# The first feed-forward product of eight layers, computed by seven products of quarters per pair of chunks

## The chip, the core and the metric

The kernel runs on one core of a Trainium2 chip. The core has a matrix engine (TensorE, in the profile PE, with its weight loads as PEld), a vector engine (VectorE, DVE), an engine for activation functions (ScalarE, ACT), a general one (GpSimd, POOL) and one that issues transfers (SyncE, SP). Each engine works through its own queue in order, and they wait for one another by semaphores. Operands lie in SBUF, products in PSUM, which has eight banks; a bank holds 512 float32 values in each of 128 partitions. The metric is the device time of one execution, in microseconds (us). Everything is float32.

## What is computed

The program is a perceiver block over 512 latent rows of 512 features: attention to 8192 context rows, eight transformer layers with an attention that is linear in length, and a feed-forward part with selected experts. The change touches the eight layers. One of them is, in the reference:

```python
def _block(x, p):
    residual = x
    q = jnp.einsum('nld,da->nla', x, Wq) + bq
    k = jnp.einsum('nld,da->nla', x, Wk) + bk
    v = jnp.einsum('nld,da->nla', x, Wv) + bv
    Q = jax.nn.elu(q) + 1.0
    K = jax.nn.elu(k) + 1.0
    KV = jnp.einsum('nsh,nsh->nh', K, v)
    Ksum = jnp.sum(K, axis=1)
    Z = 1.0 / (Q * Ksum[:, None, :] + EPS_Z)
    V = Q * KV[:, None, :] * Z
    attn = jax.nn.gelu(jnp.einsum('nla,ad->nld', V, Wo) + bo)
    x = _layernorm(attn + residual, ln1_s, ln1_b)
    residual = x
    h = jax.nn.gelu(jnp.einsum('nld,df->nlf', x, Wf1) + bf1)
    ff = jax.nn.gelu(jnp.einsum('nlf,fd->nld', h, Wf2) + bf2)
    x = _layernorm(ff + residual, ln2_s, ln2_b)
    return (x, None)
```

The line that changes is `h`: 512 tokens with 512 features each, times `Wf1` with 512 rows and 2048 columns.

## The kernel before

After the attention to the context (lines 135 to 565) the layers run one after the other (loop at line 724). Each layer has three stages on the matrix engine: the products for k, q and v with the output projection (lines 765 to 781), the first feed-forward product (line 795), and the second one (lines 805 to 811). The order of the matrix engine's instructions is that in which the code issues them; the other engines' orders are made by a scheduler that follows the data.

**The first product.** Its result is held by features: `hT[fc]`, for 16 chunks `fc`, has 128 features in the partitions and 512 tokens in the columns. The input `midT` holds the tokens' features in four slices `dc` of 128 partitions. `feature` (line 624) computes one chunk, or some columns of it: for each of the four slices a matmul with a 128x128 piece of `w_1` as weights and the tokens as moving operand, summed in PSUM. One such float32 matmul shows in the trace as two records of the matrix engine and two weight loads. `hidden` (line 786) then has ACT apply gelu from PSUM into `hT`.

**Its order.** `midT` comes into being while the product runs. The rows that the output projection leaves are normalized (`finish`, line 668), transposed by the matrix engine and copied into `midT` by ACT (`turn`, line 693), one block of 128 tokens at a time, by four calls for blocks 0 to 3. So `features` (line 631) starts with five chunks held in PSUM: of these it computes 128 tokens, or 256, as the blocks arrive, with the three remaining transposes put in between, and the other eleven chunks follow with 512 columns at a time.

**Around it.** `affine` (line 689) computes the normalized rows themselves, `mid`, on DVE: two instructions per block of tokens, right after the last `finish`. They are read by the `finish` of the second product (line 807). The second product, `returned` (line 704), takes for each block of tokens all 16 chunks of `hT` in order.

**Buffers.** PSUM is shared out as five banks for products (`mm`) and three for sums and transposes (`acc`), lines 595 and 596. The residual rows `cur` and their transposed form `curT` have two buffers each, which `mid` and `midT` take in turn; `cur` is read last by the `finish` of the output projection, `curT` by the product for v. The weights of the following stages are loaded by SP as the buffers of earlier ones come free (`layer_weights`, line 569), the rows of biases and scales by ACT's queue (line 729).

Of the kernel before, what the change touches and what calls it, by code (L numbers as in the profile page):

```python
# [8 lines left out]
F32 = mybir.dt.float32  # L9
I32 = mybir.dt.int32  # L10
AF = mybir.ActivationFunctionType
ALU = mybir.AluOpType
# [4 lines left out]
P = 128  # L17
# [3 lines left out]
TT = T // P  # L21
# [10 lines left out]
NF = DFF // P  # L32
# [8 lines left out]
C_BF1 = 112  # L41
# [4 lines left out]
R_BO, R_S1, R_B1, R_BF2, R_S2, R_B2 = range(6)  # L46
# [8 lines left out]
def perceiver_kernel(  # L55
# [3 lines left out]
    nc = tc.nc  # L59
# [17 lines left out]
    col = cpool.tile([P, NCOL], F32, name="col")  # L77
# [76 lines left out]
    def bank(name, shape=None):  # L154
        return ps_s.tile(shape or [P, BLK], F32, tag="s", name=name)
# [56 lines left out]
    k_sb, v_sb, xT, part, rows_of, trigs = {}, {}, {}, {}, {}, {}  # L212
# [118 lines left out]
    while min(met) < NCHUNK:  # L331
        p = k % NPAIR
# [261 lines left out]
    with ExitStack() as s_:  # L594
# [36 lines left out]
        def features(chunks, xT, turns, done):  # L631


            held = [(mm.tile([P, T], F32, tag="mm", name="ps"), *c) for c in chunks[:EARLY]]

            def tile_of(t, chunks_):
                for i in chunks_:
                    ps, w, c0 = held[i]
                    feature(ps, w, c0, xT, t * P, P)
                    if t % 2:  # L640
                        done(i, ps, (t - 1) * P, H)

            def half(t0, chunks_):
                for i in chunks_:
                    ps, w, c0 = held[i]
                    feature(ps, w, c0, xT, t0, H)
                    done(i, ps, t0, H)

            if 1 in turns:
                tile_of(0, (0, 1))  # L650
                turns[1]()
                tile_of(0, (2,))
                tile_of(1, (0, 1, 2))
            else:
                half(0, (0, 1, 2))
            half(0, (3,))
            turns[2]()
            half(0, (4,))
            turns[3]()
            tile_of(2, (0, 1))  # L660
            tile_of(3, (0, 1))
            half(H, (2, 3, 4))
            for i, (w, c0) in enumerate(chunks[EARLY:], EARLY):
                ps = mm.tile([P, T], F32, tag="mm", name="ps")
                feature(ps, w, c0, xT)
                done(i, ps, 0, T)

        def finish(ps, old, bias, t, eng):

            g = gpool.tile([P, D], F32, tag="g", name="g")  # L670
            nc.vector.tensor_tensor(g, ps, bias, ALU.add)  # L671
            nc.scalar.activation(g, g, AF.Gelu_apprx_tanh)  # L672
            nc.vector.tensor_tensor(g, g, old[:, t, :], ALU.add)
            mv = small.tile([P, 1, 2], F32, tag="mv1", name="mv")
            st = small.tile([P, 6], F32, tag="st", name="st")
            nc.vector.bn_stats(st, g)
            nc.vector.bn_aggr(mv[:, 0, :], st)
            r = rsqrt_of(mv[:, :, 1], 1, 1e-6)
            if eng is None:
                return g, mv[:, 0, 0:1], r  # L680
            if eng is nc.vector:
                last = nc.vector.tensor_scalar(g, g, mv[:, 0, 0:1], r, ALU.subtract, ALU.mult)
            else:
                n = small.tile([P, 1], F32, tag="nmr1", name="nmr")
                last = nc.vector.scalar_tensor_tensor(n, mv[:, 0, 0:1], -1.0, r, ALU.mult, ALU.mult)
                nc.scalar.activation(g, g, AF.Identity, bias=n, scale=r)
            return g, last

        def affine(dst, g, scale, shift):
            nc.vector.tensor_tensor(dst, g, scale, ALU.mult)  # L690
            nc.vector.tensor_tensor(dst, dst, shift, ALU.add)
# [32 lines left out]
        for l in range(NL):  # L724
            w_k, w_q, w_v, w_o, w_1, w_2 = layer_weights(l) if l else first
            row = []
            for i in range(6):
                rt = rpool.tile([P, D], F32, tag="row", name=f"row{l}_{i}", bufs=9)
                nc.scalar.dma_start(out=rt, in_=rows[l, i].partition_broadcast(P))
                row.append(rt)  # L730


            kf, ksum, qf, y, vt = {}, {}, {}, {}, {}

            def taken(i, ps, t0, n):
                ac = i % DC
                ts = slice(t0, t0 + n)
                ps = ps[:, ts]
                if i < DC:
                    if t0 == 0:  # L740
                        kf[ac] = fea.tile([P, T], F32, tag="k", name="kf")
                        ksum[ac] = small.tile([P, 3], F32, tag="ksum", name="ksum", bufs=6)
                    k = ksum[ac]
                    elu1(ps, C_BK + l * DC + ac, kf[ac][:, ts], k[:, t0 // H : t0 // H + 1])
                    if t0:
                        nc.vector.tensor_tensor(k[:, 2:3], k[:, 0:1], k[:, 1:2], ALU.add)
                elif i < 2 * DC:
                    if t0 == 0:
                        qf[ac] = fea.tile([P, T], F32, tag="q", name="qf", bufs=2)
                    elu1(ps, C_BQ + l * DC + ac, qf[ac][:, ts])  # L750
                    if t0 + n == T:
                        y[ac] = fea.tile([P, T], F32, tag="y", name="y")
                        nc.vector.tensor_scalar(y[ac], qf[ac], ksum[ac][:, 2:3], 1e-6, ALU.mult, ALU.add)
                        nc.vector.reciprocal(y[ac], y[ac])  # L754
                        nc.gpsimd.tensor_tensor(y[ac], qf[ac], y[ac], ALU.mult)  # L755
                else:
                    c = C_BV + l * DC + ac
                    kvs = small.tile([P, 1], F32, tag="kvs", name="kvs")
                    nc.vector.scalar_tensor_tensor(
                        kf[ac], ps, col[:, c : c + 1], kf[ac], ALU.add, ALU.mult, accum_out=kvs  # L760
                    )
                    nc.vector.tensor_scalar(y[ac], y[ac], kvs, None, ALU.mult)
                    vt[ac] = y[ac]

            chunks = [(w, ac * P) for w in (w_k, w_q, w_v) for ac in range(DC)]
            features(chunks, curT, turns, taken)


            mid = cpl.tile([P, TT, D], F32, tag="cur", name="mid")
            midT = cpl.tile([P, DC, T], F32, tag="curT", name="midT")  # L770
            c1, c2 = (C_S1 + l * DC, C_B1 + l * DC), (C_S2 + l * DC, C_B2 + l * DC)
            gs = {}
            for t in range(TT):
                po = acc.tile([P, D], F32, tag="acc", name=f"po_{l}_{t}")
                for ac in range(DC):
                    if t == TT - 1 and ac == 2:
                        turn(midT, gs[0], 0, *c1)
                    nc.tensor.matmul(  # L778
                        po, vt[ac][:, t * P : (t + 1) * P], w_o[:, ac, :], start=(ac == 0), stop=(ac == DC - 1)
                    )  # L780
                gs[t], last = finish(po, cur, row[R_BO], t, nc.scalar)
            turns = {t: lambda dst=midT, g=gs[t], t=t, c=c1: turn(dst, g, t, *c) for t in (1, 2, 3)}

            hT = {}

            def hidden(fc, ps, t0, n):
                if t0 == 0:
                    hT[fc] = hpool.tile([P, T], F32, tag="h", name="h")
                ts = slice(t0, t0 + n)
                c = C_BF1 + l * NF + fc  # L790
                nc.scalar.activation(  # L791
                    hT[fc][:, ts], ps[:, ts], AF.Gelu_apprx_tanh, bias=col[:, c : c + 1]
                )

            features([(w_1[fc // 4], (fc % 4) * P) for fc in range(NF)], midT, turns, hidden)

            with tc.issue_after(last.ins):
                for t in range(TT):
                    affine(mid[:, t, :], gs[t], row[R_S1], row[R_B1])

            cur = cpl.tile([P, TT, D], F32, tag="cur", name="cur")
            if l + 1 == NL:
                break
            curT = cpl.tile([P, DC, T], F32, tag="curT", name="curT")
            for t in range(TT):
                pf = returned(t, range(NF))
                gs[t], last = finish(pf, mid, row[R_BF2], t, nc.vector)
                affine(cur[:, t, :], gs[t], row[R_S2], row[R_B2])
                if t and t < 3:
                    turn(curT, gs[t - 1], t - 1, *c2)  # L810
            turns = {t: lambda dst=curT, g=gs[t], t=t, c=c2: turn(dst, g, t, *c) for t in (2, 3)}
# [265 lines left out]
```

## Time and profile before

| | us |
|---|---|
| median of 3 runs (lowest, highest) | 2690.72 (2688.86, 2693.32) |
| the profiled execution, its own time | 2689.87 |
| its span in the profile | 2688.0 |
| PE busy | 2621.7 (98% of the span) |
| DVE busy | 1482.6 (55%) |
| ACT busy | 1127.0 (42%) |
| POOL busy | 778.5 (29%) |
| first product, first layer (1298.58 to 1355.70) | 57.12 |
| second product, first layer (1355.70 to 1410.70) | 55.00 |
| next layer's k, q, v and output projection (1410.70 to 1471.40) | 60.70 |

The lower three rows are stretches of the matrix engine's work, cut at the first record of each stage. An engine's busy time is the union of its instructions; matmuls are pipelined, so the mean duration of one is longer than the distance from one to the next. "Released by" names the instruction whose semaphore ended an idle time. Over the whole program POOL works mainly in the attention to the context; in the layers it has one kind of instruction, four times a layer (line 755).

### The profile page before, as it was taken

How to read it: one execution, taken by the hardware profiler on the slowest of the kernel's cores; microseconds unless marked ns; L12 is line 12 of the kernel's file. 1: busy time of each engine (PE TensorE's matmuls, PEld its weight loads, DVE VectorE, ACT ScalarE, POOL GpSimd, SP SyncE). 2: the span in 40 equal slices, each digit the busy share in tenths (PEclk: the TensorE clock that was granted, in tenths of full speed). 3: DMA queues.
4: the chain of work that ended last, by engine and by line, in shares of the span. 5: the costliest groups of instructions: out<-in, count | busy, mean ns of one | idle time of the engine just before them, and what ended most of it. 6: DMA issues, size and time to landing. Idle time of an engine off the chain costs nothing.

```text
span 2688.0 us, 27832 instructions
## 1 busy us (share of the span) xinstructions
PE 2621.7 (98%) x9704; PEld 1264.3 (47%) x9704; DVE 1482.6 (55%) x2892; ACT 1127.0 (42%) x2125; POOL 778.5 (29%) x642
## 2 busy tenths in 40 slices
PE   8999999999999999979999999999999999999998
PEld 4433333433343333335546555455554555645544
DVE  4467677776767776876428055271461623706344
ACT  2466566565666666652314233133231331413303
POOL 0356666666765666760000000000000000100002
PEclk9999999999999999989999999999999999999999
DMA  3111111110111111105213222032221322212225
GB/s 132 48 44 40 39 37 30 53 37 27 45 42 38 34 40 40 40 7 178 76 68 103 71 90 90 31 121 90 74 90 47 115 81 86 79 63 94 68 91 202
DMA packets 98347, 187.10 MB, mean 70 GB/s; under 512 B 10336, under 2 KB 10464, under 8 KB 98208
## 3 DMA queue, kind: packets, MB, share of 16 engines
q1 hardware_dynamic: 88496, 167.29, 19.4%
q10 hardware_dynamic: 8688, 15.94, 1.8%
q0 software_dynamic: 1024, 2.10, 0.2%
q8 instruction: 77, 1.26, 0.2%
q14 instruction: 62, 0.51, 0.1%
HBM read 162.22 MB, written 1.05 MB: 61 GB/s over the span
## 4 chain that ended last, share of the span: by engine, by line
PE 71%; DVE 17%; ACT 5%; issue 4%; POOL 2%; DMA 0%; SPq 0%; DVEq 0%; POOLq 0%; ACTq 0%
PE ps L626 20%; PE pf L708 16%; PE pv L259 7%; PE pk L230 6%; PE po L455 6%; PE pc L374 6%; DVE y L754 4%; DVE sc L434 3%; PE po L778 3%; ACT sc L377 2%; ACT sc L435 1%; POOL es L445 1%; DVE qf L620 1%; PE pt L218 1%; DVE mx L383 1%
## 5 line engine op out<-in xcount | busy, mean ns | idle before, releaser
L445 POOL TENSOR_TENSOR es<-es,sc 128x1024 f32<-128x1024 f32 x222 | 524.9, 2365 | 114.7 <-ACT sc L435 103.7
L626 PE MATMUL ps<-midT,w 128*128 128x512 f32 (+2 forms) x1664 | 451.7, 431 | 0.0
L708 PE MATMUL pf<-w,h 128*128 128x512 f32 x1024 | 444.5, 593 | 0.0
L755 POOL TENSOR_TENSOR y<-qf,y 128x512 f32<-128x512 f32 x32 | 47.0, 1468 | 1207.7 <-DVE y L754 1207.7
L435 ACT ACTIVATE sc<-sc 128x1024 f32<-128x1024 f32 x272 | 288.1, 1063 | 242.9 <-DVE sc L434 231.7
L383 DVE TENSOR_TENSOR mx<-pc,mx 128x512 f32<-128x512 f32 x448 | 283.1, 683 | 191.8 <-ACT sc L377 191.6
L671 DVE TENSOR_TENSOR g<-pf,row 128x512 f32<-128x512 f32 x32 | 22.1, 691 | 645.0 <-PE pf L708 645.0
L626 PEld LDWEIGHTS ps<-midT,w 128*128 128x128 f32 x1664 | 267.7, 191 | 177.3 <-issue 166.4
L377 ACT COPY sc<-pc 128x512 f32<-128x512 f32 x544 | 284.1, 599 | 92.8 <-PE pc L374 77.4
L434 DVE TENSOR_TENSOR sc<-sc,mbc 128x1024 f32<-128x1024 f32 x272 | 319.0, 1207 | 3.7 <-PE mbc L411 2.2
L708 PEld LDWEIGHTS pf<-w,h 128*128 128x128 f32 x1024 | 193.1, 190 | 235.7 <-issue 235.6
L374 PE MATMUL pc<-qT,k 64*128 64x512 f32 x1088 | 288.0, 621 | 2.8 <-ACT v L265 1.3
L455 PE MATMUL po<-sc,v 128*64 128x512 f32 x1088 | 265.0, 608 | 0.2 <-DVE mx L383 0.2
L230 PE MATMUL pk<-xn,wkv 128*128 128x512 f32 x544 | 254.9, 613 | 7.0 <-ACT v L265 2.9
L259 PE MATMUL pv<-wkv,xn 128*128 128x512 f32 x544 | 249.6, 602 | 6.2 <-DVE sin L241 3.3
L791 ACT ACTIVATE h<-ps,col 128x256 f32<-128x256 f32 (+1 forms) x168 | 97.3, 584 | 301.0 <-PE ps L626 301.0
L672 ACT ACTIVATE g<-g 128x512 f32<-128x512 f32 x64 | 40.0, 625 | 394.3 <-DVE g L671 394.3
L374 PEld LDWEIGHTS pc<-qT,k 64*128 64x128 f32 x1088 | 101.0, 187 | 183.8 <-issue 79.7
L230 PEld LDWEIGHTS pk<-xn,wkv 128*128 128x128 f32 x544 | 100.5, 194 | 150.2 <-issue 107.8
L259 PEld LDWEIGHTS pv<-wkv,xn 128*128 128x128 f32 x544 | 98.5, 190 | 140.6 <-issue 106.7
L455 PEld LDWEIGHTS po<-sc,v 128*64 128x64 f32 x1088 | 67.8, 137 | 145.9 <-issue 123.1
L626 PE MATMUL ps<-curT,wk 128*128 128x256 f32 (+1 forms) x664 | 123.4, 343 | 2.4 <-ACT curT L699 1.7
(170 smaller groups left out, 2707.4 us busy)
## 6 DMA issues: line engine op xcount, KB each, us to landing
w<-in_wf SPq DMA_DIRECT2D x64, 1024.0 KB, 5.4
k<-cos SPq DMA_DIRECT2D x272, 64.0 KB, 2.0
cb<-in_cx SPq DMA_DIRECT2D x62, 256.0 KB, 3.5
row<-in_rows ACTq DMA_DIRECT2D x48, 256.0 KB, 3.4
f<-in_f SPq DMA_DIRECT2D x10, 1024.0 KB, 6.2
tg<-in_trig SPq DMA_DIRECT2D x16, 512.0 KB, 3.8
wk<-in_wk SPq DMA_DIRECT2D x8, 1024.0 KB, 5.4
wq<-in_wq SPq DMA_DIRECT2D x8, 1024.0 KB, 5.4
```

The costliest lines, as they stand in the source:

```text
L230: nc.tensor.matmul(pk, wkv[:, 0, dc, j * P : (j + 1) * P], xT[b, dc], start=(dc == 0), stop=(dc == DC - 1))
L259: nc.tensor.matmul(pv, xT[b, dc][:, t * P : (t + 1) * P], wkv[:, 1, dc, :], start=(dc == 0), stop=(dc == DC - 1))
L374: nc.tensor.matmul(pc[h], k_sb[b, p][hs, o : o + P], qT[hs, p, :], start=True, stop=True)
L377: copied[0] = nc.scalar.copy(sc[:, h, :], pc[h])
L383: behind[0] = nc.vector.tensor_tensor(mx[u][:, h, :], pc[h], mx[u][:, h, :], ALU.max)
L434: nc.vector.tensor_tensor(sc, sc, mbc[u], ALU.subtract)
L435: nc.scalar.activation(sc, sc, AF.Exp)
L445: nc.gpsimd.tensor_tensor(es[u], es[u], sc, ALU.add)
L455: nc.tensor.matmul(po[u][h * HD : (h + 1) * HD, :], v_sb[b, p][:, t * P + h * HD : t * P + (h + 1) * HD], scores[u, i][:, h, :], start=(i ...
L626: nc.tensor.matmul(ps[:, t0 : t0 + n], w[:, dc, c0 : c0 + P], xT[:, dc, t0 : t0 + n], start=(dc == 0), stop=(dc == DC - 1),)
L708: nc.tensor.matmul(pf, hT[fc][:, t * P : (t + 1) * P], w_2[fc // 4][:, fc % 4, :], start=(fc == 0), stop=(fc == NF - 1),)
L754: nc.vector.reciprocal(y[ac], y[ac])
```

## The change

Two chunks of 128 features are taken together as a pair `p`, and the product is cut into quarters: the two chunks `i`, two halves of the 512 input features (two slices `k` each), and two halves of the 512 tokens. With A(i,j) the weights of chunk i and feature half j, and B(i,j) the input of feature half i and token half j, a pair needs eight products A(i,j) B(j,t), each of 256 tokens and two slices. The change computes them by seven products, in Winograd's form of Strassen's scheme:

- weight sums, four per pair: S1 = A10 + A11, S2 = S1 - A00, S3 = A00 - A10, S4 = A01 - S2
- token sums, four per layer: T1 = B01 - B00, T2 = B11 - T1, T3 = B11 - B01, T4 = B10 - T2
- products: p1 = A00 B00, p2 = A01 B10, p3 = S4 B11, p4 = A11 T4 (its sign is taken care of in T4), p5 = S1 T1, p6 = S2 T2, p7 = S3 T3
- seven additions from PSUM per pair, which give the two chunks' halves.

In the code `o0` and `o1` are the pair's two tiles of `hT`, which hold sums on the way and then, in place, gelu's result. The weight sums run on GpSimd and lie in the buffer of `cur`, two pairs' worth; the token sums run on DVE (T1, T2, T4) and GpSimd (T3), each in two blocks of 128 tokens, and lie in the buffer of `curT`. p1 and p2 share a bank of `mm`, and p4 is written over p2; p6 and p7 of a pair share a bank of `acc`, p5 and p3 another (for the first two pairs: p5 of both, p6 of both, p7 of both, p3 of both). `affine` is moved from the stage's start to behind pairs 2 to 5, one block of tokens behind each.

```diff
+        class Seven:
...
+            def weight_sums(self, p, which):
+                if 2 * p >= len(self.chunks):
+                    return
+                s1, s2, s3, s4 = (self.sw[:, p % 2, i] for i in range(4))
+                of = {
+                    1: (s1, self.a(p, 1, 0), self.a(p, 1, 1), ALU.add),
+                    2: (s2, s1, self.a(p, 0, 0), ALU.subtract),
+                    3: (s3, self.a(p, 0, 0), self.a(p, 1, 0), ALU.subtract),
+                    4: (s4, self.a(p, 0, 1), s2, ALU.subtract),
+                }
+                for i in which:
+                    nc.gpsimd.tensor_tensor(*of[i])
+
+            def token_sums(self, t):
+
+                t1, t2, t3, t4 = (self.sx[:, i, :, t * P : (t + 1) * P] for i in range(4))
+                b11, b12, b21, b22 = (self.b(i, j, t * P, P) for i in range(2) for j in range(2))
+                nc.vector.tensor_tensor(t1, b12, b11, ALU.subtract)
+                nc.vector.tensor_tensor(t2, b22, t1, ALU.subtract)
+                nc.gpsimd.tensor_tensor(t3, b22, b12, ALU.subtract)
+                return nc.vector.tensor_tensor(t4, b21, t2, ALU.subtract)
+
+            def product(self, ps, lhs, rhs):
+                for k in range(2):
+                    nc.tensor.matmul(ps, lhs[:, k], rhs[:, k], start=(k == 0), stop=(k == 1))
+
+            def bank(self, *halves):
+
+                b = acc.tile([P, 2, H], F32, tag="acc", name="pw")
+                for j, h in enumerate(halves):
+                    self.ps[h] = b[:, j, :]
+
+            def p12(self, p, t0=0, n=H):
+
+                if t0 == 0:
+                    self.held[p] = mm.tile([P, 2, H], F32, tag="mm", name="ps")
+                p1, p2 = (self.held[p][:, j, :] for j in range(2))
+                for j, ps in enumerate((p1, p2)):
+                    self.product(ps[:, t0 : t0 + n], self.a(p, 0, j), self.b(j, 0, t0, n))
+                if t0 + n == H:
+                    o0, o1 = self.o[p] = self.tiles(p)
+                    nc.scalar.copy(o1[:, :H], p1)
+                    nc.vector.tensor_tensor(o0[:, :H], o1[:, :H], p2, ALU.add)
+                    self.out(2 * p, o0[:, :H])
+
+            def p6(self, p, t0=0, n=H):
+                self.product(self.ps[p, 6][:, t0 : t0 + n], self.sw[:, p % 2, 1], self.sx[:, 1, :, t0 : t0 + n])
+                if t0 + n == H:
+                    o0, o1 = self.o[p]
+                    nc.vector.tensor_tensor(o0[:, H:], o1[:, :H], self.ps[p, 6], ALU.add)
+
+            def p7(self, p):
+                self.product(self.ps[p, 7], self.sw[:, p % 2, 2], self.sx[:, 2])
+                o0, o1 = self.o[p]
+                nc.vector.tensor_tensor(o1[:, :H], o0[:, H:], self.ps[p, 7], ALU.add)
+
+            def p5(self, p, t0=0, n=H):
+                self.product(self.ps[p, 5][:, t0 : t0 + n], self.sw[:, p % 2, 0], self.sx[:, 0, :, t0 : t0 + n])
+
+            def add5(self, p):
+                o0, o1 = self.o[p]
+                nc.vector.tensor_tensor(o1[:, H:], o1[:, :H], self.ps[p, 5], ALU.add)
+                nc.vector.tensor_tensor(o0[:, H:], o0[:, H:], self.ps[p, 5], ALU.add)
+
+            def p3(self, p):
+                self.product(self.ps[p, 3], self.sw[:, p % 2, 3], self.b(1, 1))
+                o = self.o[p][0][:, H:]
+                nc.vector.tensor_tensor(o, o, self.ps[p, 3], ALU.add)
+                self.out(2 * p, o)
+
+            def p4(self, p):
+                ps = self.held[p][:, 1, :]
+                self.product(ps, self.a(p, 1, 1), self.sx[:, 3])
+                o = self.o[p][1]
+                last = nc.vector.tensor_tensor(o[:, :H], o[:, :H], ps, ALU.add)
+                self.out(2 * p + 1, o)
+                return last
...
-            features([(w_1[fc // 4], (fc % 4) * P) for fc in range(NF)], midT, turns, hidden)
-
+            s7 = Seven(
+                [(w_1[fc // 4], (fc % 4) * P) for fc in range(NF)], midT, cur, curT, hidden_tiles, hidden
+            )
             with tc.issue_after(last.ins):
-                for t in range(TT):
-                    affine(mid[:, t, :], gs[t], row[R_S1], row[R_B1])
+                for i in range(1, 5):
+                    for p in range(2):
+                        s7.weight_sums(p, (i,))
+            for p in range(2):
+                s7.p12(p, 0, P)
+            turns[1]()
+            s7.p12(2, 0, P)
+            for p in range(3):
+                s7.p12(p, P, P)
+            s7.p12(3)
+            turns[2]()
+            s7.token_sums(0)
+            s7.p12(4)
+            turns[3]()
+            s7.token_sums(1)
+            for i in (5, 6):
+                s7.bank((0, i), (1, i))
+                for p in range(2):
+                    (s7.p5 if i == 5 else s7.p6)(p, 0, P)
+            for f in (s7.p5, s7.p6):
+                for p in range(2):
+                    f(p, P, P)
+            s7.bank((0, 7), (1, 7))
+            for p in range(2):
+                s7.p7(p)
+                s7.add5(p)
+                s7.weight_sums(p + 2, (1, 2, 3))
+            for p in range(2):
+                s7.p4(p)
+            s7.bank((0, 3), (1, 3))
+            for p in range(2):
+                s7.p3(p)
+                s7.weight_sums(p + 2, (4,))
+            for p in range(2, NF // 2):
+                if p > 2:
+                    s7.p12(p + 2) if p + 2 < NF // 2 else None
+                s7.bank((p, 6), (p, 7))
+                s7.p6(p)
+                s7.p7(p)
+                s7.bank((p, 5), (p, 3))
+                s7.p5(p)
+                s7.add5(p)
+                s7.weight_sums(p + 2, (1, 2, 3))
+                s7.p3(p)
+                s7.weight_sums(p + 2, (4,))
+                last = s7.p4(p)
+                if p - 2 < TT:
+                    with tc.issue_after(last.ins):
+                        affine(mid[:, p - 2, :], gs[p - 2], row[R_S1], row[R_B1])
```

The lines left out are the two views `a` and `b` of weights and tokens, the constructor, and `hidden`, which now applies gelu in place to a piece of `hT`, not from PSUM.

More of the change, by code (lines that the diff above doesn't have):

```diff
@@ L666, in features, with __init__, a, b @@
                 done(i, ps, 0, T)
+        class Seven:
+            def __init__(self, chunks, xT, sums_w, sums_x, tiles, out):
+                self.chunks, self.xT, self.tiles, self.out = chunks, xT, tiles, out
+                self.sw = sums_w.rearrange("p t d -> p (t d)").rearrange(
+                    "p (b s k m) -> p b s k m", b=2, s=4, k=2
+                )
+                self.sx = sums_x.rearrange("p c t -> p (c t)").rearrange("p (s k t) -> p s k t", s=4, k=2)
+                self.held, self.ps, self.o = {}, {}, {}
+            def a(self, p, i, j):
+                w, c0 = self.chunks[2 * p + i]
+                return w[:, 2 * j : 2 * j + 2, c0 : c0 + P]
+            def b(self, i, j, t0=0, n=H):
+                return self.xT[:, 2 * i : 2 * i + 2, j * H + t0 : j * H + t0 + n]
+            def weight_sums(self, p, which):
[62 more added lines that the diff above has]
+                return last
@@ L784, in perceiver_kernel, with hidden @@
             hT = {}
-            def hidden(fc, ps, t0, n):
-                if t0 == 0:
-                    hT[fc] = hpool.tile([P, T], F32, tag="h", name="h")
[L789 to L793, printed above, removed]
-            features([(w_1[fc // 4], (fc % 4) * P) for fc in range(NF)], midT, turns, hidden)
-            with tc.issue_after(last.ins):
-                for t in range(TT):
-                    affine(mid[:, t, :], gs[t], row[R_S1], row[R_B1])
+            def hidden(fc, h):
+                c = C_BF1 + l * NF + fc
+                nc.scalar.activation(h, h, AF.Gelu_apprx_tanh, bias=col[:, c : c + 1])
@@ new lines, in hidden_tiles @@
+            def hidden_tiles(p):
+                for fc in (2 * p, 2 * p + 1):
+                    hT[fc] = hpool.tile([P, T], F32, tag="h", name="h")
+                return hT[2 * p], hT[2 * p + 1]
+            s7 = Seven(
+                [(w_1[fc // 4], (fc % 4) * P) for fc in range(NF)], midT, cur, curT, hidden_tiles, hidden
+            )
+            with tc.issue_after(last.ins):
+                for i in range(1, 5):
+                    for p in range(2):
+                        s7.weight_sums(p, (i,))
```

## The prediction

> **What bounds the kernel now.** I first cut a layer into stages and read each engine's busy time there. Columns: us of the stage; PE, PEld, DVE, ACT, POOL busy with instructions; granted clock, DMA share, GB/s.
>
> ```profile
> 1471.42:1528.53 57.11, 57.11 (x221) 34.75 (x221) 8.97 (x24) 18.37 (x37) 0.00 (x0) 1.00 0.26 88
> ```
>
> In the first feed-forward product PE is busy for all of the stage at full clock, DVE for 9 of 57 us, POOL never. So the stage is as long as PE's work in it, and less work there is less time, as long as PE still never stops. Next I read what a record of PE costs by width, from the groups of the layers and from gelu's starts, which follow finished chunks.
>
> ```profile
> L626 PE MATMUL ps<-midT,w 128*128 128x512 f32 x704 | 303.4, 592 | 0.0
> ...
> L626 PE MATMUL ps<-midT,w 128*128 128x128 f32 x640 | 79.1, 280 | 0.0
> ...
> L626 PE MATMUL ps<-midT,w 128*128 128x256 f32 x320 | 73.1, 379 | 0.0
> ```
> ```profile
> 1487.35 0.47 ACT L791 ACTIVATE h<-ps,col 128x256 f32<-128x256 f32 x1 [1.25 <-PE ps L626]
> ...
> 1489.08 0.47 ACT L791 ACTIVATE h<-ps,col 128x256 f32<-128x256 f32 x1 [1.25 <-PE ps L626]
> ...
> 1494.24 0.69 ACT L791 ACTIVATE h<-ps,col 128x512 f32<-128x512 f32 x1 [2.96 <-PE ps L626]
> ...
> 1497.67 0.69 ACT L791 ACTIVATE h<-ps,col 128x512 f32<-128x512 f32 x1 [2.75 <-PE ps L626]
> ```
>
> Eight records (four matmuls) of 512 columns lie in 3.43 us, 0.429 us each; eight of 256 in 1.73, 0.216 each: half the columns cost half. For 128 columns, 79.1/640 = 0.124, and 1.96/16 = 0.122 at the stage's start; I take 0.1215. The rows' means (592, 379, 280 ns) hold the pipeline's length too and are not used.
>
> Last I read what a stop of PE costs, at the output projection, where it waits for DVE.
>
> ```profile
> 1458.10 0.49 DVE L762 TENSOR_SCALAR y<-y,kvs 128x512 f32<-128x512 f32 x1
> 1458.64 0.30 PEld L778 LDWEIGHTS po<-wo,y 128*128 128x128 f32 x2 [0.96 <-DVE y L762]
> 1459.18 0.19 PEld L778 LDWEIGHTS po<-wo,y 128*128 128x128 f32 x1 [0.24 <-issue]
> 1459.61 0.19 PEld L778 LDWEIGHTS po<-wo,y 128*128 128x128 f32 x1 [0.24 <-issue]
> 1459.81 0.69 DVE L671 TENSOR_TENSOR g<-po,row 128x512 f32<-128x512 f32 x1 [1.22 <-PE po L778]
> ```
>
> DVE ends at 1458.59, the weight load starts 0.05 later. The third load starts with the second matmul, at 1459.18, so the first matmul streamed from 1459.18 - 0.43 = 1458.75, 0.11 after the load: **0.16 us from DVE's end to PE's streaming**. The last matmul has been fed at 1459.61 and DVE reads it at 1459.81: **0.20 us from PE to DVE**.
>
> **PE's work.** Now, per layer: 88 records of 512, 40 of 256, 80 of 128 columns and three transposes of 0.44: 37.75 + 8.64 + 9.72 + 1.32 = 57.4 (57.11 measured, 0.6% off). After: eight pairs of seven products, two slices, two records each are 224 records of 256; 40 of them are cut in two (p1 and p2 of pairs 0 to 2, p5 and p6 of pairs 0 and 1): 184 x 0.216 + 80 x 0.1215 + 1.32 = 50.8. Removed: **6.65 us a layer**, 53.2 in eight.
>
> **The waits that it adds.** In the changed program's order of instructions I followed each wait of PE to the instruction that it waits for. Waits on weight sums, token sums and transfers are dealt with below. But p7's first matmul waits for DVE's addition that reads p6, and p3's for the second addition of `add5`, which reads p5: the halves of one bank are not written by PE while DVE still reads the other half. Both stand straight behind the product that DVE has to read, so PE has nothing to do in between. In each layer there are nine waits for one addition (p7 of pairs 2 to 7; p6, p7 and p3 of pair 1, each behind pair 0's in the same bank) and six for `add5` (p3 of pairs 2 to 7).
>
> The trace has no addition of 128x256 from PSUM. The nearest:
>
> ```profile
> L863 DVE TENSOR_TENSOR bd<-pp,cst 128x512 f32<-128x512 f32 x4 | 2.8, 692 | 4.1 <-PE pp L861 4.1
> ...
> L964 DVE TENSOR_TENSOR inn<-pti,col 128x128 f32<-128x128 f32 x8 | 2.3, 290 | 8.5 <-PE pti L959 8.5
> ```
>
> Between 0.29 and 0.69; on the line through both, 0.42, which I take as 256 lies between the two widths. A second DVE addition right behind comes 0.08 sooner than its duration (`affine`'s pairs of 0.68 take 1.28). So:
> - one addition: 0.20 + 0.42 + 0.16 = 0.78 us of standing PE
> - `add5`: both additions need p5 (the one of p7 is done during p5): 0.20 + 0.42 + 0.34 + 0.16 = 1.12.
>
> A layer has 9 x 0.78 + 6 x 1.12 = **13.7 us** of it. Two smaller terms: pair 6 follows pair 5 without p1 and p2 of a later pair in front, so the first instruction of the last `affine` stands before the addition of p6 in DVE's queue: p4's addition at 0.20 to 0.63, `affine` to 1.27, the addition to 1.70, PE at 1.86 and not 1.65: 0.21. And p6's second block of tokens needs T2, which comes behind ACT's copies of `midT`: from 1479.4, with p1 of pair 3 and block 2 transposed, ACT's queue holds a copy of p1 (0.37, between 265 ns for 128 and 585 for 512 columns), four copies into `midT` (two take 0.81), a gelu (0.47), and the same again for block 3: 4.9 us, to 1484.4, so T2 at 1485.0; PE has six small products until then, to 1484.9, so 0.26 with the restart.
>
> What lies behind the waiting matmuls: all of PE's later products, as its queue is in order, hence gelu on ACT and the second product. Nothing makes up for it, since the second product (55.0 us) is PE's too.
>
> **What is hidden.** Weight sums on POOL: 128x512 takes 1277 ns (L246), 128x1024 2366 (L443), so 2.13 ns an element and 0.73 us for 256; upper bound 1.47, the 512-column row of L755. Four per pair are 2.9 us (5.9 at the bound) of a pair's 14 x 0.431 + 0.78 + 1.12 = 7.9 us: covered. The first eight run from 1473.9, when the last `finish` has read `cur`, to 1479.8; PE wants the first at 1482.0. DVE's seven additions (2.9 us) and `affine` (1.3) fit into 7.9 as well, ACT's copy and gelus (0.37 + 2 x 0.47 + 0.69 = 2.0) too. The last pair's gelus are covered by the 14 matmuls (12 us) that the second product does before it reads them. `affine`'s delay to pairs 2 to 5 holds back two transfers of rows in ACT's queue until pair 6; the gelus behind them are wanted 12 us later. SP's queue waits for the weights' last readers as before; the loads (5.4 us) have tens of us.
>
> One thing between POOL and DVE is not hidden for certain. The same DVE form, beside POOL's L755 and without it:
>
> ```profile
> 1437.81 1.37 DVE L620 TENSOR_SCALAR qf<-m 128x512 f32<-128x512 f32 x1
> 1439.21 0.48 DVE L753 TENSOR_SCALAR y<-qf,ksum 128x512 f32<-128x512 f32 x1
> ```
>
> T2 and T3 of the second block start together, on DVE and POOL. If DVE is held off until T3 (0.73) is done, p6 comes that much later; if not, nothing: I take half, 0.37. The Trainium skill, SBUF — State Buffer, section "Who interferes with whom", says that a DVE instruction with two SBUF inputs and a reading GpSimd instruction exclude one another, and that with one SBUF input there is no contention: by it the term would be 0 or 0.73, and the additions from PSUM untouched. The additions from PSUM I leave at 0.42, since L383, the same form with 512 columns, takes 683 ns beside a busy POOL and L671 690 beside an idle one.
>
> A page of the Trainium skill speaks against the change itself: PSUM — Partial Sum Buffer, section "PSUM bank collisions raise a hardware error", wants PSUM guarded by bank, since two engines in one bank go wrong even at different columns. No row here shows that; by it the fifteen waits can't be had for nothing in these banks, and without it the sum would be the gain alone.
>
> **Sum.** 13.7 + 0.21 + 0.26 + 0.37 = 14.6 added, 6.65 removed: 7.9 us a layer, 63.5 in eight. On the profiled execution's own 2689.87 (span 2688.0 and 1.9 around it) that is 2753.4; the median of the runs is 0.85 above it: **2754**.
>
> **Rivals.**
> - The waits are covered, and PE never stops: 2690.7 - 53.2 = 2637.5, faster. For it: PE's idle time in the stage is 0.0 now, and DVE is free five sixths of it. Against: it decides at 6.65/15 = 0.44 us a wait, and 0.36 of that is the way to DVE and back, which leaves 0.08 for an addition of at least 0.29. Chance 0.04.
> - Additions at the row of 128 columns, 0.29: waits of 0.65 and 0.86, 11.0 us a layer without the small terms, 4.4 net: 2691 + 35 = 2726, slower still. Against: twice the columns. Chance 0.06.
> - POOL late as well: sums of 1.47 end at 1485.7, T3's two blocks at 1487.2 and 1488.6, while p7 of pair 0 is due at 1486.9: 1.75 us a layer, 2754 + 14 = 2768. It decides from 1.3 us a sum. For it: L755's 1468 ns, pieces of 128 columns in the operands, which no row has. Against: L246 and L443. Chance 0.09.
> - Half-width matmuls cost PE more than half, so that nothing is saved: excluded by 0.216 against 0.429.
>
> **Numbers.** The forecast has 0.80, and 0.01 is left for no change. Additions at 0.69 would make waits of 1.05 and 1.66, 19.4 + 0.84 - 6.65 = 13.6 a layer, 2799; the line through both rows makes that end unlikely. The range goes from the lower row (2728) to half the way from the forecast to the upper one and past POOL's case: 2728 to 2785. A difference under 0.2% (5 us) can't be told from none. Faster 0.04, same 0.02, slower 0.94.
>
> **What would show it.** In the changed profile the stage lasts some 65 us, PE has 15 gaps of 0.8 to 1.1 us in it, ended by DVE's additions of p6 and of `add5`; records of 256 columns still 0.216 apart; POOL's sums at 0.73 us, never the end of a gap. Wrong, if the gaps are under 0.44 us or are ended by POOL, or the additions don't take 0.42.

## The result, and the profile after

| | before | after |
|---|---|---|
| median (lowest to highest), us | 2691.82 (2688.86 to 2693.32), 4 runs | 2751.25 (2750.24 to 2751.89), 4 runs |
| ratio of the medians, 95% interval | 1 | 1.0222 (1.0204 to 1.0240) |
| span of the profiled execution, us | 2688.0 | 2749.7 |
| PE busy, us (share of the span) | 2621.7 (98%) | 2599.9 (95%) |

The changed kernel is slower by 59 us; the prediction was 2754, with a range of 2728 to 2785. One execution of a later run (the third bank taken later) had a granted clock of 0.946 and took 2709.10 us, and is left out of that run's figures.

The time is lost in the first product alone. From the start of one layer's second product to the start of the next layer's, the trace has 172.83 us before (1355.70 to 1528.53) and 180.55 after (1362.85 to 1543.40): 7.72 more, and 8 x 7.72 = 61.8 is the difference of the spans (61.7). Within that period, the stretch up to a weight load near the start of the next output projection (at 1458.64 before, at 1465.75 after) is 102.94 us before and 102.90 after. The rest went from 69.89 to 77.65. In it the remainder of the output projection takes 12.61 us in both, so the 7.76 more are the first product's.

The changed kernel's stage, as the stretch was shown before (us of the stage; PE, PEld, DVE, ACT, POOL busy with instructions; granted clock, DMA share, GB/s):

```profile
1478.20:1543.24 65.04, 54.62 (x278) 44.38 (x276) 34.68 (x88) 22.29 (x48) 20.77 (x28) 1.00 0.23 78
```

PE had no idle time there before. Now the stage is 65 us (64.9 from its first matmul at 1478.36) and PE is idle in 10.4 of them by its records, at the same full clock. What ended that idle time is in the groups of PE in the changed kernel:

```profile
L712 PE MATMUL pw<-curT,cur 128*128 128x256 f32 x640 | 162.0, 388 | 30.0 <-DVE h L737 25.9 <-DVE h L742 4.1
...
L712 PE MATMUL ps<-midT,w 128*128 128x256 f32 x320 | 75.6, 379 | 0.0
L712 PE MATMUL pw<-midT,cur 128*128 128x256 f32 x256 | 70.1, 396 | 49.0 <-POOL cur L699 29.9 <-DVE h L750 15.0 <-DVE h L755 4.1
L712 PE MATMUL ps<-curT,w 128*128 128x256 f32 x256 | 64.4, 379 | 0.0
...
L712 PE MATMUL pw<-curT,cur 128*128 128x128 f32 x256 | 33.5, 282 | 4.2 <-DVE h L737 4.1
```

All seven products share line 712, so they are told apart by their operands. `pw<-curT,cur` are p5, p6 and p7 (token sums times weight sums), `pw<-midT,cur` is p3, `ps<-midT,w` are p1 and p2, `ps<-curT,w` is p4. The products whose result goes into `ps` have not waited (0.2 us in all, in a row of 128 columns that is not shown). The idle time stands in front of products into `pw`, the banks of `acc` that are shared by halves. Line 737 is the addition that reads p6, 742 the one that reads p7, 749 and 750 are the two of `add5`, and 755 reads p3.

One releaser contradicts the prediction: 29.9 us in front of p3 are put down to POOL's weight sums (line 699). Here is pair 3 of one layer in the changed kernel (pairs count from 0), in order of time; first PE (start, length, operands, records, and the idle time before with its releaser). The rows `ps<-midT,w` are p1 and p2 of pairs 5 and 6, which the program computes ahead:

```profile
1506.63 1.89 PE L712 MATMUL ps<-midT,w 128*128 128x256 f32 x8
1508.36 1.03 PE L712 MATMUL pw<-curT,cur 128*128 128x256 f32 x4
1509.89 1.99 PE L712 MATMUL pw<-curT,cur 128*128 128x256 f32 x8 [0.51 <-DVE h L737]
1512.83 1.10 PE L712 MATMUL pw<-midT,cur 128*128 128x256 f32 x4 [0.94 <-POOL cur L699]
1513.76 1.03 PE L712 MATMUL ps<-curT,w 128*128 128x256 f32 x4
1514.63 1.89 PE L712 MATMUL ps<-midT,w 128*128 128x256 f32 x8
```

then DVE's additions of the same pair, and POOL's sums for a later one:

```profile
1509.42 0.42 DVE L737 TENSOR_TENSOR h<-h,pw 128x256 f32<-128x256 f32 x1
1511.06 0.42 DVE L742 TENSOR_TENSOR h<-h,pw 128x256 f32<-128x256 f32 x1 [1.22 <-PE pw L712]
1511.93 0.42 DVE L749 TENSOR_TENSOR h<-h,pw 128x256 f32<-128x256 f32 x1 [0.44 <-PE pw L712]
1512.26 0.41 DVE L750 TENSOR_TENSOR h<-h,pw 128x256 f32<-128x256 f32 x1
```
```profile
1511.11 1.59 POOL L699 TENSOR_TENSOR cur<-w 128x256 f32<-128x256 f32 x2 [4.30 <-PE pw L712]
```

The lines read so. p6 begins at 1508.36 and its four records are fed in 4 x 0.216 = 0.86, so until 1509.22. Line 737 reads it from 1509.42 (0.20 later) until 1509.84, and p7 begins at 1509.89. p7 and p5 are eight records that last 1.99 where eight without a stop last 1.89, so another 0.10 is lost on restarting. The stop of PE is 1.53 - 0.86 + 0.10 = **0.77 us**.

p5 is fed at 1509.89 + 0.10 + 1.73 = 1511.72, the two additions run from 1511.93 to 1512.67, and p3 begins at 1512.83, again with a slower restart (1.10 against 1.03). That stop is 2.94 - 1.73 - 0.10 + 0.07 = **1.18 us**. The idle time in brackets is shorter than these stops (0.51 and 0.94) as it counts from the ends of the records, which hold the pipeline's length as well. From one `ps<-midT,w` to the next it is 8.00 us, of which the 28 records in between are 6.04.

As to the releaser: two of POOL's sums end at 1512.70, line 750 at 1512.67, and p3 at 1512.83 stands behind both. But the sums that run there are those of pair 5. p3 of pair 3 needs pair 3's S4, which ended at 1501.34. Whether POOL holds p3 up in some other way is a matter for a run.

### The profile page after: what moved, and what is told of

The parts are those of the page before. It is cut to its first block, busy times and chain, and to the rows that moved or that the text cites. A ratio compares the mean times of both kernels' runs of the same rounds, so it can differ in the third digit from the quotient of the medians.

```text
span 2749.7 us, 29895 instructions
## 1 busy us (share of the span) xinstructions
PE 2599.9 (95%) x10152; PEld 1340.2 (49%) x10152; DVE 1690.7 (61%) x3388; ACT 1159.3 (42%) x2213; POOL 982.5 (36%) x914
## 4 chain that ended last, share of the span: by engine, by line
PE 64%; DVE 20%; ACT 7%; issue 5%; POOL 4%; DMA 0%; ACTq 0%; DVEq 0%; POOLq 0%; SPq 0%
PE pf L806 16%; PE pw L712 8%; PE pv L259 7%; PE po L455 6%; PE pk L230 6%; PE pc L374 6%; DVE y L852 4%; PE ps L626 4%; PE ps L712 4%; DVE sc L434 3%; PE po L876 2%; POOL es L445 2%; ACT sc L377 2%; ACT sc L435 1%; ACT midT L797 1%
## 5 line engine op out<-in xcount | busy, mean ns | idle before, releaser
L886 ACT ACTIVATE h<-h,col 128x256 f32<-128x256 f32 (+1 forms) x192 | 109.7, 579 | 322.2 <-DVE h L755 213.3
L712 PE MATMUL pw<-curT,cur 128*128 128x256 f32 (+1 forms) x896 | 194.2, 358 | 34.3 <-DVE h L737 30.0
L712 PEld LDWEIGHTS pw<-curT,cur 128*128 128x128 f32 x896 | 146.2, 190 | 72.0 <-DVE h L737 42.8
L699 POOL TENSOR_TENSOR cur<-w 128x256 f32<-128x256 f32 x128 | 94.3, 739 | 227.7 <-PE pw L712 106.7
```

Source lines behind the costliest of these rows:

```text
L712: nc.tensor.matmul(ps, lhs[:, k], rhs[:, k], start=(k == 0), stop=(k == 1))
```

## The experiments

Theory: PE stops because two consecutive products lie in the halves of one bank, and the second waits until DVE has read the first. First rival: the stops before p3 are POOL's, as the profile has it. Second rival: seven products of half the width with all their additions are slower whatever the banks. Each kernel was timed beside the kernel before on the same chip (medians 2689.97, 2689.42 and 2691.00 us there). Diffs are against the changed kernel unless another is named.

**p7 in a bank of its own**, for pairs 2 to 7; p5 and p3 still share one.

```diff
-                s7.bank((p, 6), (p, 7))
+                s7.bank((p, 6))
                 s7.p6(p)
+                s7.bank((p, 7))
                 s7.p7(p)
```

> Pairs 2 to 7 of the changed kernel (2751.25): p6 and p7 get a bank of their own each; p5 and p3 still share one. Theory (the loss is PE waiting for DVE to read the other half of a bank): six waits a layer go, each 0.77 us in the changed kernel's trace (p6 to p7 1.53 us apart, 0.86 of it work, and 0.10 at the restart), 6 x 0.77 x 8 = 37, so 2714; p3's waits stay at 1.18. Rival (POOL's weight sums hold PE up, as the profile names them at p3's waits in pairs 2 to 5): p7's waits go all the same, 2714, but not p3's. Rival (half-width products and DVE's reads slow PE in general): no change, 2751.

Measured 2716.65 us, ratio 1.0096 (1.0081 to 1.0111). 34.6 us less for 48 stops is 0.72 each, against 0.77 read from the trace; the runs of one kernel lie 2 to 5 us apart, which is up to 0.1 a stop. PE's idle time released by line 737 fell from 30.0 us to 4.1, which is pair 1's; the 29.9 released by line 699 and 15.0 by line 750 stayed as they were.

**Every one of p6, p7, p5 and p3 in a bank of its own**, for pairs 2 to 7. This costs no PSUM: the three banks of `acc` are then taken in turn by four products instead of two at a time.

```diff
                 s7.p7(p)
-                s7.bank((p, 5), (p, 3))
+                s7.bank((p, 5))
                 s7.p5(p)
                 s7.add5(p)
                 s7.weight_sums(p + 2, (1, 2, 3))
+                s7.bank((p, 3))
                 s7.p3(p)
```

> As the run before it, and p5 and p3 of pairs 2 to 7 have a bank each too, so that three banks go round and a product writes a bank whose reader was done two products ago. Theory: p3's six waits a layer go as well, 6 x 1.18 x 8 = 57, so 2714 - 57 = 2657, faster than the kernel before the change. Rival (POOL's sums end p3's waits in pairs 2 to 5): four of the six stay, 4 x 1.18 x 8 = 38 more, 2695. Rival (PE slowed in general): 2751.

Measured 2658.67 us, ratio 0.9886 (0.9869 to 0.9902): faster than the kernel before. The step from the first run is 58.0 us for 48 stops, 1.21 each, against 1.18 from the trace. Pair 3 of a layer on PE in this kernel (columns as above):

```profile
1492.45 1.89 PE L712 MATMUL ps<-midT,w 128*128 128x256 f32 x8
1494.17 2.75 PE L712 MATMUL pw<-curT,cur 128*128 128x256 f32 x12
1496.76 1.03 PE L712 MATMUL pw<-midT,cur 128*128 128x256 f32 x4
1497.63 1.03 PE L712 MATMUL ps<-curT,w 128*128 128x256 f32 x4
```

p6, p7 and p5 now run as one row of twelve records, p3 follows without a stop, and the pair takes 6.04 us, all of it work. POOL's sums are all there still, and none of PE's idle time in these products is released by POOL any more. That is against both rivals; a run without some of POOL's sums tests the first directly.

**The weight sums issued while pairs 2 to 7 are computed left out**, with the changed kernel's banks. These are, exactly, the sums of pairs 4 to 7, and these pairs' products use the sums that pairs 2 and 3 left in the buffer; the sums of pairs 0 to 3 are made as before.

```diff
-                s7.weight_sums(p + 2, (1, 2, 3))
                 s7.p3(p)
-                s7.weight_sums(p + 2, (4,))
```

> The changed kernel with its banks as they are, without the weight sums of pairs 2 to 7 on POOL: these pairs are multiplied with the sums of pairs 0 and 1. Theory: POOL is named at p3's waits only because its next sum, for which nobody waits there, happens to end 0.03 us after DVE's second addition of p5; the waits stay and are now put down to DVE: 2751, within 3. Rival (POOL's sums end p3's waits in pairs 2 to 5): four waits of 1.18 a layer go, 38 in all, 2713.

Measured 2749.43 us, ratio 1.0220 (1.0205 to 1.0235): 1.8 below 2751.25, which the runs' spread covers. p7 and p3 of pair 3, and p3 of pair 4, on PE in this kernel:

```profile
1509.15 1.99 PE L712 MATMUL pw<-curT,cur 128*128 128x256 f32 x8 [0.51 <-DVE h L737]
1512.08 1.10 PE L712 MATMUL pw<-midT,cur 128*128 128x256 f32 x4 [0.94 <-DVE h L750]
...
1519.98 1.13 PE L712 MATMUL pw<-midT,cur 128*128 128x256 f32 x4 [0.84 <-DVE h L750]
```

The gaps in front of p3 are all still there, and now they are put down to line 750. So the sums that ran at the time did not make the stops. They are not quite the same, though. In pairs 2 and 3, whose own sums are still made, the gap is 0.94 as before. In pairs 4 to 7, whose sums are left out, it is 0.84 with a restart of 1.13: p3 begins 2.84 after p7, and the stop is 2.84 - 1.73 - 0.10 + 0.10 = 1.11 us, not 1.18. Of PE's idle time, 42.0 us stand at line 750 here, where 15.0 + 29.9 = 44.9 stood at both names before. Newly made sums thus go with 0.07 us of a stop of 1.18, and 32 x 0.07 = 2.2 us is about what the run gained. It is not POOL's being busy beside PE: in the changed kernel pairs 6 and 7, for which no sums run any more, have 0.94 too. Why a p3 with newly made sums starts later is not shown.

**Another order instead of other banks**: pairs 2 to 7 keep the shared banks, but between a product and the one that shares its bank there is another (p6, p5, p7, then p4, p3).

```diff
                 s7.p6(p)
-                s7.p7(p)
                 s7.bank((p, 5), (p, 3))
                 s7.p5(p)
+                s7.p7(p)
                 s7.add5(p)
                 s7.weight_sums(p + 2, (1, 2, 3))
+                last = s7.p4(p)
                 s7.p3(p)
                 s7.weight_sums(p + 2, (4,))
-                last = s7.p4(p)
```

> The changed kernel with its banks shared as they are, but in pairs 2 to 7 PE's order is p6, p5, p7, p4, p3 and not p6, p7, p5, p3, p4. Theory (a wait costs what the products in between don't cover): behind p6 comes p5, 0.86 us, and p7 waits 0.78 at most for the addition of p6, so its stop goes. p3 waits for three additions behind p7, 0.20 + 0.42 + 0.04 + 0.42 + 0.34 + 0.16 = 1.58, of which p4 covers 0.86, so 0.72 is left of 1.18. Saved 6 x (0.77 + 0.46) x 8 = 59, so 2692, about the kernel before the change. Rival (the loss comes from sharing banks as such, by slower reads or writes): the order changes nothing, 2751.

Measured 2699.41 us over nine runs, ratio 1.0031 (1.0021 to 1.0042), 7 more than expected. A pair on PE in this kernel:

```profile
1511.55 2.75 PE L712 MATMUL pw<-curT,cur 128*128 128x256 f32 x12
1514.14 1.03 PE L712 MATMUL ps<-curT,w 128*128 128x256 f32 x4
1515.70 1.10 PE L712 MATMUL pw<-midT,cur 128*128 128x256 f32 x4 [0.53 <-DVE h L750]
1516.64 1.89 PE L712 MATMUL ps<-midT,w 128*128 128x256 f32 x8
...
1525.51 1.10 PE L712 MATMUL pw<-curT,cur 128*128 128x256 f32 x4 [0.17 <-DVE h L737]
```

One product (0.86 us) between two halves of a bank covers the whole of p7's stop (0.77), so p6, p5 and p7 run as twelve records. In front of p3, DVE now has the addition of p7 to do as well, ahead of the two of `add5`; 1.56 - 0.86 + 0.07 = 0.77 is left with p4 in between. The last line is pair 6's p7, which still waits: no product of a later pair stands in front of it, and DVE was given an `affine` first. Its stop is 2.06 - 1.73 + 0.07 = 0.40 us; it and the 0.05 more at each p3 are 8 x 0.40 + 48 x 0.05 = 5.6 of the 7.4 us above the expectation, and the rest is not assigned. The order took 51.8 us off the changed kernel, own banks 92.6.

**The same for pairs 0 and 1**, on top of the own banks: p6 and p7 of one pair share a bank, not the same product of both pairs, and p3 has its own.

```diff
-            for i in (5, 6):
-                s7.bank((0, i), (1, i))
-                for p in range(2):
-                    (s7.p5 if i == 5 else s7.p6)(p, 0, P)
+            s7.bank((0, 5), (1, 5))
+            for p in range(2):
+                s7.p5(p, 0, P)
+            for p in range(2):
+                s7.bank((p, 6), (p, 7))
+                s7.p6(p, 0, P)
...
-            s7.bank((0, 7), (1, 7))
...
-            s7.bank((0, 3), (1, 3))
             for p in range(2):
+                s7.bank((p, 3))
                 s7.p3(p)
```

> As the run before it, and at the stage's start p6 and p7 are put together by pair, not by product, and p3 of pairs 0 and 1 have a bank each: PE writes the other pair's bank while DVE reads. Theory: of three waits of 0.77 a layer some 0.3 is left (p7 of pair 0 comes 0.49 after its p6), so 2.0 x 8 = 16 less, 2641; PE then stands still in the stage for under half a microsecond a layer, and its work alone would give 2638. Rival (PE slowed in general): no gain from it. Rival (POOL): 2695 - 16 = 2679.

Measured 2649.58 us, ratio 0.9848 (0.9833 to 0.9862); I had missed 8.6 us. PE at the stage's start in this kernel:

```profile
1478.81 2.47 PE L712 MATMUL pw<-curT,cur 128*128 128x128 f32 x20 [0.82 <-ACT midT L797]
1481.44 1.96 PE L712 MATMUL pw<-curT,cur 128*128 128x256 f32 x8 [0.16 <-POOL cur L699]
```

The edit takes three banks of `acc` at once, and the third still held the last transposed block, which ACT was copying into `midT`. It is the same mechanism with another reader. The stop is 0.86 us: p6 of pair 1 begins at 1478.81, and the twelve records of 0.1215 before it begin at 1476.49. That is 8 x 0.86 = 6.9 us of the miss; the other 1.7 was there in the run before (2658.67, where 2657 had been expected). The small stop behind it, at p7 of pair 0, is the one that the expectation had at some 0.3.

**The third bank taken later**, on top of that: p6 and p7 of pair 1 get their bank only when all blocks are there.

```diff
-            for p in range(2):
-                s7.bank((p, 6), (p, 7))
-                s7.p6(p, 0, P)
-            for f in (s7.p5, s7.p6):
-                for p in range(2):
-                    f(p, P, P)
+            s7.bank((0, 6), (0, 7))
+            s7.p6(0, 0, P)
+            for p in range(2):
+                s7.p5(p, P, P)
+            s7.p6(0, P, P)
+            s7.bank((1, 6), (1, 7))
+            s7.p6(1)
```

> e3_start_too (2649.58) was 8 us above its expectation of 2641. Its trace has one stop of 0.82 us a layer at p6 of pair 1, put down to ACT's copies into midT. Here that product takes its bank later and in one piece: p6 of pair 0 and the second blocks of p5 come first. Theory (the third acc bank is still the last transpose's, which ACT reads until then): the stop goes, some 0.3 a layer comes in where p5's second block waits for T1; 0.8 to 1.0 a layer less, 6 to 8 in all, 2642 to 2644. Rival (that product waits for T2 or the weight sums, not for its bank): T2 is awaited all the same, no gain, 2650.

Measured 2644.12 us (median of four, 2642.34 to 2646.28), ratio 0.9831 (0.9818 to 0.9844), where 2642 to 2644 had been expected. That p6 of pair 1 no longer waits is seen in the next run, which has the same order.

**T3 on DVE, not on POOL**, on top of that.

```diff
-                nc.gpsimd.tensor_tensor(t3, b22, b12, ALU.subtract)
+                nc.vector.tensor_tensor(t3, b22, b12, ALU.subtract)
```

> As e5_start_bank, with T3 on DVE and not on POOL. In the changed kernel DVE's T4 takes 0.73 us on the mean, beside POOL's T3 (0.97), where T1 and T2, the same form, take 0.42. Theory (DVE and POOL hold one another up when both read two operands from SBUF): T4 falls to 0.42 and POOL's sums lie at 0.73; DVE has one addition of 0.42 more per block. T4 is not what PE waits for, so the time is that of e5_start_bank, within 3 us. Rival (T4 is long because it follows T2 directly): T4 stays at 0.73.

Measured 2643.01 us (2641.21 to 2644.70), ratio 0.9827 (0.9814 to 0.9841). It can't be told from the run before it (1.1 us), and T4 fell to 0.42, as expected (last section). It is the best kernel of the study, 108 us below the change and 46 below the kernel before. Its stage (columns as above) and the stop that is left at its start:

```profile
1463.78:1515.30 51.52, 51.06 (x274) 45.44 (x273) 35.11 (x91) 22.53 (x48) 18.87 (x26) 1.00 0.30 98
```
```profile
1476.43 4.20 PE L712 MATMUL pw<-curT,cur 128*128 128x128 f32 x24 [0.45 <-DVE curT L705]
```

The stretch takes in 0.3 us of the second product, whose first record is at 1515.00, so the stage is 51.2 us. Seven products with all their sums and additions take that long where eight took 57.1. PE waits in it only for T1's second block, for 0.5 us.

## Why the prediction was right, step by step

**The work removed.** It said 57.4 to 50.8 us a layer, 6.65 less. The last kernel, which has the same 28 records per pair, has a stage of 51.2 us with one stop of 0.5: 50.7 of work. In the changed kernel 64.9 less the stops of 14.2 (below) is 50.7 as well. So the saving was there too, and was more than given back. But it is 6.4, not 6.65: the stage before took 57.1, as the prediction had measured, and its sum went on with 57.4. Records of 256 columns are 0.216 us apart in all the rows above.

**The waits for one addition.** The prediction had 0.20 to DVE, 0.42 for the addition and 0.16 back, 0.78 in all. The trace has 0.20, 0.42 and 0.15; giving p7 its own bank removed 0.72 a stop. The addition had been placed on the line between the rows of 128 and 512 columns, 0.42, and the changed kernel's groups on DVE have it:

```profile
L737 DVE TENSOR_TENSOR h<-h,pw 128x256 f32<-128x256 f32 x64 | 26.9, 421 | 14.4 <-PE pw L712 13.5
L750 DVE TENSOR_TENSOR h<-h,pw 128x256 f32<-128x256 f32 x64 | 26.5, 414 | 0.0
```

**The waits for `add5`.** Predicted 1.12, measured 1.18 in the trace and 1.21 by the run: 0.06 too small, six times a layer 0.36 us. The part that was off lies between DVE's end and PE: p3 begins 0.16 after line 750's end and loses another 0.07 on restarting, 0.23, where p7 needs 0.15. In the run without the later weight sums it is 0.05 + 0.10 = 0.15 for pairs 4 to 7 and the stop is 1.11, so the way back from DVE was right. What the sum left out goes with the newly made weight sums; the prediction had POOL's sums at nothing here.

**The small terms, which were wrong.** 0.26 for T2 held up behind ACT's copies and 0.37 for T2 and T3 in each other's way were not there. PE ran its 28 small products, from p5's first block to p6's second, without a stop:

```profile
1489.07 3.42 PE L712 MATMUL pw<-curT,cur 128*128 128x128 f32 x28
```

The prediction had T2's block done too late for the last of them. It was done at 1491.70, 0.29 before p6's second block began at 1489.07 + 24 x 0.1215 = 1491.99: ACT's last copy ended at 1491.24, 12.9 us after the stage's first matmul where the prediction had 13.1, DVE began 0.03 later and not some 0.2, and T2 took 0.43 us beside T3, as it began just before T3 (below). The 0.21 for the last `affine` in front of pair 6's addition came out as 0.08 (p6 to p7 in 1.61 us, not 1.53). Pair 2 lost 0.10 there too, which was not foreseen and whose cause is open.

**The sum.** Predicted 13.7 + 0.84 - 6.65 = 7.9 a layer, measured 7.72. With the stops and the work as measured it is 9 x 0.77 + 6 x 1.18 + 0.18 - 6.4 = 7.8. The errors went both ways: the waits for `add5` (0.36 a layer) and the work removed (0.25) made the forecast too low, the small terms (0.66) and the waits for one addition (0.09) too high. The mechanism and its main terms were right; that the number came within 2.8 us is in part luck. Of the 2.8, some 1.7 are the layers' (8 x 0.21). The rest is the step from the profiled execution to the median, which had been put at 0.85 up and was 0.22 down. The ends of the range are not what its rows give: the lower row is worked out as 2726 in the rivals, and half the way to 2799 is 2777.

**What was to be seen.** A stage of some 65 us: 64.9. Fifteen gaps: the program's order has fifteen a layer, and PE shows 15 x 8 = 120 stops released by lines 737, 742, 750, 755 and 699 together. "Never the end of a gap" for POOL's sums failed as a statement on the profile, where 32 of the gaps carry POOL's name. As a statement on the cause it held but for 0.07 us a stop: the gaps stay without the sums that are named there. The first eight sums were said to run from 2.5 to 8.4 us after the stage's start (1473.9 to 1479.8 against 1471.42), behind the last `finish`; each in fact needs only the block of `cur` that it overwrites, and in the changed kernel they ran one by one from 1469.23, 9.1 us before the stage's first product at 1478.36, to 1482.83. PE waited for none.

**The rivals.** "The waits are covered" at 2637.5 us failed by the banks, not by the seven products: the last kernel is within 5.5 us of it. Smaller additions and slow POOL sums are out by the additions' 0.42 and the sums' 0.73 us.

## What to carry to other kernels

In this program two products in the halves of one PSUM bank made PE wait for whoever read the first half: the way to the reader, its work and the way back, even if the reader was idle most of the time. The wait is one that the program sets by its semaphores; no run here lets PE write one half while the other is read, so what the chip would make of that is not shown. Give consecutive products different banks in turn, or put another product between them, and count the stops before a saving of matmuls: here fifteen stops of 0.8 to 1.2 us a layer turned a gain of 6.4 us into a loss of 7.7. Where a profile names a releaser, look whether the program's wait needs that very instruction; leaving it out is the test.

## What the runs showed of the hardware that was not expected

POOL and DVE hold each other up where DVE reads two operands from SBUF, and almost for the other's whole instruction. The token sums in the changed kernel (T3 on POOL; L706 is T2, L708 T4) and in the last one (T3 on DVE), groups of 128x256:

```profile
L708 DVE TENSOR_TENSOR curT<-midT,curT 128x256 f32<-128x256 f32 x16 | 11.6, 727 | 0.3
L706 DVE TENSOR_TENSOR curT<-midT,curT 128x256 f32<-128x256 f32 x16 | 6.8, 425 | 8.8 <-ACT midT L797 8.8
...
L707 POOL TENSOR_TENSOR curT<-midT 128x256 f32<-128x256 f32 x16 | 15.5, 968 | 60.3 <-ACT midT L797 60.3
```
```profile
L708 DVE TENSOR_TENSOR curT<-midT,curT 128x256 f32<-128x256 f32 x16 | 6.7, 419 | 0.0
```

T4 takes 727 ns beside T3 and 419 without it; T3 takes 968 on POOL where the weight sums take some 730; T2, which starts 0.04 us before T3, loses nothing (425). The three for one block of tokens in the changed kernel (start and length on DVE, then on POOL):

```profile
1491.27 0.43 DVE L706 TENSOR_TENSOR curT<-midT,curT 128x256 f32<-128x256 f32 x1 [0.44 <-ACT midT L797]
1491.73 0.83 DVE L708 TENSOR_TENSOR curT<-midT,curT 128x256 f32<-128x256 f32 x1
```
```profile
1491.31 0.97 POOL L707 TENSOR_TENSOR curT<-midT 128x256 f32<-128x256 f32 x1 [1.10 <-ACT midT L797]
```

The three take 1.29 us, from 1491.27 to 1492.56, where one after another they would take 0.42 + 0.73 + 0.42 = 1.57. T3 ends 0.58 after T2's end and T4 0.28 after T3's end, each some 0.14 sooner than if it had begun only when the one before it ended. The Trainium skill, SBUF — State Buffer, section "Who interferes with whom", states an exclusive lock between the two engines for such operations. The trace agrees that there is a hold-up, that the instruction which starts first loses nothing, and that the additions with one operand in PSUM don't have it (line 749 takes 0.42 beside POOL's sums). The prediction gave the page's rule for one SBUF input without its condition, that the instruction is outside the two-port modes; for these additions that made no difference. The records overlap by those 0.14 us each; whether that is outside a lock, at an instruction's start or end, or against one, no run here shows. The price in this kernel is small: with T3 on DVE the time was 1.1 us lower, inside what these runs can tell apart.
